# Layer weights' places lent to gathered keys, and a thinner interleave of attention at the layer border, in a two-layer graph transformer

## The chip, the cores and the metric

The kernel runs on one core of a Trainium2 chip. The metric is the device time of one launch in microseconds (us); the time of a version is the median of its runs. A profile is one execution recorded by the hardware profiler. PE is the matrix engine (TensorE), DVE the vector engine, ACT the scalar engine, POOL the general engine (GpSimd), which also issues the gathers, and SP the engine that issues most plain transfers.

## What is computed

Two transformer layers over 2708 nodes of 512 features, 8 heads of 64, a feed-forward part of width 2048. Attention goes only to the neighbours that a sparse adjacency matrix names. Each layer does this (the two layers have weights of their own):

```
mask = adj.astype(jnp.float32) + jnp.eye(n, dtype=jnp.float32)
q = (h @ Wq.T + bq).reshape(n, N_HEADS, D_K)
k = (h @ Wk.T + bk).reshape(n, N_HEADS, D_K)
v = (h @ Wv.T + bv).reshape(n, N_HEADS, D_K)
scores = jnp.einsum('nhd,mhd->hnm', q, k) / jnp.sqrt(jnp.float32(D_K))
scores = jnp.where(mask[None, :, :] == 0, jnp.float32(-1000000000.0), scores)
attn = jax.nn.softmax(scores, axis=-1)
ctx = jnp.einsum('hnm,mhd->nhd', attn, v).reshape(n, D_MODEL)
attn_out = ctx @ Wo.T + bo
h1 = _layer_norm(h + attn_out, ln1_g, ln1_b)
ff = jax.nn.relu(h1 @ W1.T + b1) @ W2.T + b2
h2 = _layer_norm(h1 + ff, ln2_g, ln2_b)
```

## The kernel before

**Stages.** The kernel first turns the adjacency matrix into a list of at most 24 neighbours for each node, while PE computes the keys and values of layer 0 (kept as rows of 1024 numbers in the table `kv_d[0]`) and then the queries (`first_queries`). Nodes are sorted by the length of their lists, so each of the 22 tiles of 128 nodes has its own number of list places (`CAPS`, 22 down to 3; the last tile has 20 nodes). From there on the work goes by 11 blocks of two tiles (`blocks`; the loop variable is k), once for layer 0 and once for layer 1. The stretch between the two layers, in which layer 1's first queries are computed, is called the border here.

**Two strands.** PE's strand is dense: for each block, `attended` (the context transposed, times Wo, first norm), `turned` (the result transposed to `hT`), `feed_forward` (16 steps f, each four matmuls into `pf`, a relu on ACT into `ft`, and the second product into `a`), the second norm, and in layer 0 `keys_values`, which makes the next layer's keys and values of the block. The other strand is attention, which PE does not touch. `loads` gathers neighbour rows with POOL's indirect transfers (L982), two list places, a *chunk*, into one tile `kv` of 8 KB a partition. `Tile.weights` multiplies a chunk by the queries and sums by head on DVE (L1019, L1025, into `sc`); `Tile.weigh` takes exponentials on ACT (L1038, into `p`), scales the values half on ACT (L1045), half on DVE (L1051), and adds them up on DVE (L1058, into `acc`). L1058 is the last reader of a chunk's tile, so it frees the place for a later gather. `sums` and `divided` end a tile's attention (L1081, and L1089 on ACT into `cx`). 

**What sets the order.** `attend` is a generator, one step a chunk: step j takes the gathered chunk j, writes out its weights, and then `weigh` of chunk j-1, `sums` of j-2 and `divided` of j-3. `loads` runs EARLY = 3 chunks ahead of that in the program. `advance(x)` adds x to a credit and runs steps while credit is left; the main loop calls it once for each f (0.62 in layer 0, 0.72 in layer 1), and `through(k + 1)` at f = 10 runs whatever is missing of the next block's attention in one go. The orders of PE, ACT and SP are those of the program text throughout. POOL's is that of the text up to the end of block 0 of layer 0; DVE's during `first_queries` and at the border. In the rest a scheduler orders DVE and POOL when the kernel is built, by its own idea of when things are ready. Every engine's stream is fixed then: an engine waits at an instruction whose inputs are not there, and everything behind it waits too.

**Places in memory.** The chunks have KVB = 5 tiles with the tag `kv`. `keys_values` takes one of these five for the rows that it scatters (`kvs`). Each weight matrix has one place of its own in the pool `wts`: `wq`, `wk`, `wv` are 4 x 512 numbers a partition, 8 KB, the size of a chunk's tile. Wq of layer 0 is last read by `first_queries`; Wq of layer 1 is loaded into the place at (k, f) = (3, 2) of layer 0 on SP's queue, and first read at the border. Wk and Wv of layer 1 are loaded in block 0 of layer 0, and last read by the last `keys_values`, at the start of the border.

**The border.** PE computes queries: two right after layer 0, two after the last keys and values, four more of tiles loaded beforehand, six of tiles streamed in (`now.queries`), then `through(0)` and `attended` of block 0, then two more. Before each of the four and the six stands `advance(0.5)`, so attention chunks of layer 1 lie between the queries' evictions (L1226, from PSUM into `qs`) in DVE's stream. The queries' sums `q`, the transposes `tp` and the product `o` share three PSUM tiles (tag `g`) in turn: PE can begin the fourth only when DVE has emptied the first. `qs` has three places in the tag `row`, freed when SP has stored it to `q_d`.

Of the kernel before, what the change touches and what calls it, by code (L numbers as in the profile page):

```python
# [8 lines left out]
F32 = mybir.dt.float32  # L9
# [9 lines left out]
P = 128  # L19
DM = 512  # L20
# [3 lines left out]
NC = DM // P  # L24
# [12 lines left out]
SLOTS = 2  # L37
QB = 3
LAG = 3
KVB = 5  # L40
# [431 lines left out]
def by_edges(ctx: ExitStack, tc: tile.TileContext, x, xT, adj, layers, out, good):  # L472
# [13 lines left out]
    NL = len(layers)  # L486
# [10 lines left out]
    wts = ctx.enter_context(tc.tile_pool(name="wts", bufs=1))  # L497
# [8 lines left out]
    all_made = []  # L506
    at = None
# [22 lines left out]
    def matrix(w, name, tag, by=None):  # L530
        src = chunked(w[name])
        t = wts.tile([P, src.shape[1], src.shape[2]], F32, tag=tag, name=tag)
        if by:
            by.dma_start(out=t, in_=src)
            return t
        k = max(1, src.shape[1] // 4)
        for c in range(0, src.shape[1], k):
            nc.sync.dma_start(out=t[:, c : c + k, :], in_=src[:, c : c + k, :])
        return t
# [11 lines left out]
    def turned_row(col, name, scale):  # L551

        t = rows.tile([P, DM], F32, tag=name, name=name)
        dg = dn.tile([P, NC, P], F32, tag="row", name="dg", bufs=3)
        for c in range(NC):
            nc.vector.tensor_scalar(
                dg[:, c, :], ident, col[:, c : c + 1], scale, ALU.mult, ALU.mult
            )
        yield t
        pr = ps.tile([P, DM], F32, tag="g", name="pr")  # L560
        for c in range(NC):
            nc.tensor.matmul(pr[:, c * P : (c + 1) * P], ones, dg[:, c, :], start=True, stop=True)
        nc.vector.tensor_copy(t, pr)
# [8 lines left out]
    def finish(steps):  # L572
        for _ in steps:
            pass
# [6 lines left out]
    def size(g):  # L581
        return min(P, N - g * P)
# [398 lines left out]
    def gather(to, table, s):  # L981
        nc.gpsimd.indirect_dma_start(  # L982
            out=to,
            out_offset=None,
            in_=table[:, :],
            in_offset=bass.IndirectOffsetOnAxis(ap=s, axis=0),
            bounds_check=N - 1,
            oob_is_err=False,
        )
# [12 lines left out]
    def chunks_of(g):  # L1002
        S = CAPS[g]
        k = (S + SLOTS - 1) // SLOTS
        cuts = [-(-S * i // k) for i in range(k + 1)]
        return [(g, a, b - a) for a, b in zip(cuts, cuts[1:])]

    class Tile:
# [75 lines left out]
        def divided(self):  # L1084
# [6 lines left out]
                )  # L1091
            return cx

    def loads(n):

        ready = []
        for g, s0, c in (chunk for g in order for chunk in chunks_of(g)):
            r = size(g)
            kv = at.tile([P, SLOTS, 2 * DM], F32, tag="kv", name="kv", bufs=KVB)
            for s in range(s0, s0 + c):  # L1100
                gather(kv[:r, s - s0, :], kv_d[n], idx[:r, g, s : s + 1])
            ready.append(kv)
            if len(ready) > EARLY:
                yield ready.pop(0)
        yield from ready
# [267 lines left out]
    NB = len(blocks)  # L1373
# [50 lines left out]
    def advance(more):  # L1424

        nonlocal credit
        credit = min(credit + more, 1.5)
        while credit > 0 and len(got) < CXB - 1:
            cost = next(ahead, None)
            if cost is None:  # L1430
                break
            credit -= cost

    def through(k):

        while blocks[k][-1] not in got:
            next(ahead)

    got = {}
    ahead = attend(0, got)  # L1440
# [37 lines left out]
    for n in range(NL):  # L1478
        last = n == NL - 1
        nxt = None if last else Layer(n + 1, layers[n + 1])  # L1480
        if n > 0:
            streamed = now.queries(order[8 : 2 * AHEAD])
            got = {}
            ahead = attend(n, got)
            with tc.manual_schedule(engines={mybir.EngineType.DVE}):
                for _ in range(2):
                    now.query(*pool.pop(0))
                next(ahead)
                next(streamed)
                while pool:  # L1490
                    advance(0.5)
                    now.query(*pool.pop(0))
                for i in range(2 * AHEAD - 10):
                    advance(0.5)
                    next(streamed)
                through(0)
                early[n] = now.attended(blocks[0], got)
                next(early[n])
                for _ in blocks[0]:
                    next(early[n])  # L1500
                finish(streamed)
            now.load_w2(NFC // 2 - 1)
        *_, hs = early[n]
        hT = now.turned(blocks[0], hs)
        turning = projecting = None
        in_order = ExitStack()
        if n == 0:
            in_order.enter_context(tc.manual_schedule(engines={mybir.EngineType.Pool}))
        for k, block in enumerate(blocks):
            more = k + 1 < NB  # L1510
            asking = iter(())
            if n > 0 and k + AHEAD < NB:
                asking = now.queries(blocks[k + AHEAD])
            for f, zs in enumerate(now.feed_forward(block, hs, hT)):
                if f == NFC:
                    break
                if f in (5, 6, 7, 8) and behind:
                    next(behind)
                if more and f == 10 + (k + n == 0):
                    through(k + 1)  # L1520
                    projecting = now.attended(blocks[k + 1], got)
                    next(projecting)
                if more and f == 11 + (k + n == 0):
                    for hs_next in projecting:
                        advance(0.5 if k else 0.0)
                advance(PACE[n] if k else 1.1 if f < 11 else 0.4)
                if f in (0, 3, 7, 9):
                    next(asking, None)
                if more and f == NFC - 1:
                    finish(asking)  # L1530
                    hT = now.turned(blocks[k + 1], hs_next)
                if k == 0 and len(now.w1) < NFC // 2 and f % 2 == 0:
                    now.load_w1(len(now.w1), nc.scalar)
                    now.load_w2(len(now.w2), nc.scalar)
                if n > 0 and (k, f) == (0, 2):
                    now.load_second(1, temp)
                if not last:
                    if (k, f) == (0, 10):
                        now.load_next()
                        now.kv = [matrix(nxt.w, "Wk", "wk", nc.scalar)]  # L1540
                    if (k, f) == (0, 13):
                        now.kv.append(matrix(nxt.w, "Wv", "wv", nc.scalar))
                    if (k, f) == (3, 2):
                        now.wq = matrix(nxt.w, "Wq", "wq")
                    if f == 1 and k in (1, 3):
                        i, name, scale = (1, "bk", 1.0) if k == 1 else (0, "bq", DK**-0.5)
                        turning = turned_row(now.cols[i], name, scale)
                        rows_of = now if k == 1 else nxt
                        setattr(rows_of, name, next(turning))
                    if f == 3 and k in (1, 3):  # L1550
                        finish(turning)
                if not last and not more:
                    if f % 2:
                        nxt.load_w1(f // 2)
                        if f > 2:
                            nxt.load_w2(f // 2 - 1)
                    if f == 6:
                        nxt.load_first()
                        nxt.load_second(0, temp)
                    if f == 7:  # L1560
                        finish(ahead)
                        pool += nxt.preloaded(order[:8], temp)
            in_order.close()
            if not last:
                behind = now.keys_values(block, zs)
            if more:
                hs = hs_next
        finish(ahead)
        if last:
            checked()  # L1570
        else:
            nxt.wq = now.wq
            for _ in range(2):
                nxt.query(*pool.pop(0))
            nxt.kept()
            for g in order[:2]:
                own[g] = asked(n + 1, g)
            finish(behind)
            behind = None
            now = nxt  # L1580
# [63 lines left out]
```

## Time and profile before

| | before |
|---|---|
| median of 3 runs | 1966.08 us (1964.01 to 1967.41) |
| the profiled execution's own time | 1964.63 us |
| its span | 1962.9 us |
| mean granted PE clock | 0.989 |

Busy time by stretch, in us, from a table of stretches:

| stretch | what runs | length | PE | DVE | ACT | POOL | PE clock |
|---|---|---|---|---|---|---|---|
| 0 to 264 | lists, keys and values, queries | 264 | 258.2 | 178.2 | 104.8 | 79.6 | 1.00 |
| 264 to 345 | layer 0, block 0 | 81 | 69.0 | 63.2 | 40.2 | 43.3 | 0.89 |
| 345 to 1130 | layer 0, the rest | 785 | 771.8 | 487.1 | 379.4 | 310.9 | 1.00 |
| 1130 to 1230 | border | 100 | 92.3 | 47.6 | 19.6 | 26.8 | 0.97 |
| 1230 to 1830 | layer 1, with attention | 600 | 590.2 | 496.7 | 367.3 | 322.4 | 1.00 |
| 1830 to 1962.9 | layer 1, the end | 132.9 | 119.7 | 27.9 | 22.6 | 13.7 | 0.96 |

A row is read like this: of the 81 us of layer 0's block 0, PE was busy for 69.0, and over that stretch it was granted 0.89 of its full clock, so its matmuls there were also slower than elsewhere. DVE is the fullest of the other engines in layer 1 (83%), and none of the others is full over a whole stretch.

### The profile page before, as it was taken

The page shows a single profiled execution, that of the slowest core. Times are in us where ns is not written, and L with a number is a line of the kernel's source. Part 1 is how long each engine was busy: PE and PEld are TensorE (multiplying, and loading weights), DVE is VectorE, ACT ScalarE, POOL GpSimd, SP SyncE. Part 2 cuts the span into 40 slices and gives each one's busy share as a digit, 9 for nine tenths or more (in the row PEclk, how much of TensorE's full clock was granted, in tenths as well). Part 3 has the DMA queues.
Part 4 walks back from the last instruction along what each step waited for, and adds up shares of the span by engine and source line. Part 5 has one row for each costly group of instructions (what it writes and reads, how often), then busy time and mean ns, then how long its engine had stood idle before and what let it go on. Part 6 is the DMA issues. An engine that isn't in the chain of part 4 may idle for free. (4 is left out here: it accounts for less than half of the span.)

```text
span 1962.9 us, 20872 instructions
## 1 busy us (share of the span) xinstructions
PE 1901.0 (97%) x6162; PEld 1100.6 (56%) x6162; DVE 1300.8 (66%) x2142; ACT 933.8 (48%) x3219; POOL 796.8 (41%) x710
## 2 busy tenths in 40 slices
PE   8999988999999999999999998999999999999997
PEld 4444444565565655566556643556666566666664
DVE  5884587685867869659442036888688988877421
ACT  4660254564555655547332112756456765755410
POOL 3114635453555535425310022555347655644210
PEclk9999999999999999999999999999999999999998
DMA  9998766455655556546310646856455766554000
GB/s 327 352 311 307 258 211 235 161 166 189 202 161 199 188 186 227 161 150 204 130 43 27 230 162 215 298 174 217 153 177 198 247 214 209 186 190 154 34 11 13
DMA packets 131486, 366.92 MB, mean 187 GB/s; under 512 B 16668, under 2 KB 36988, under 8 KB 128654
## 3 DMA queue, kind: packets, MB, share of 16 engines
q0 software_dynamic: 69120, 246.35, 37.9%
q1 hardware_dynamic: 53332, 99.66, 14.9%
q10 hardware_dynamic: 8910, 19.48, 2.6%
q8 instruction: 50, 0.82, 0.2%
q14 instruction: 74, 0.61, 0.1%
HBM read 314.62 MB, written 50.83 MB: 186 GB/s over the span
## 5 line engine op out<-in xcount | busy, mean ns | idle before, releaser
L982 POOL DMA_INDIRECT kv<-kv_d,idx x420 | 546.1, 1300 | 475.9 <-DVE acc L1058 319.1
L1284 PE MATMUL a<-w,ft 128*128 128x512 f32 (+1 forms) x1408 | 669.9, 601 | 10.8 <-ACT ft L1304 9.5
L1296 PE MATMUL pf<-hT,w 128*128 128x256 f32 (+1 forms) x2816 | 636.3, 373 | 13.2 <-ACT ft L1304 8.8
L1296 PEld LDWEIGHTS pf<-hT,w 128*128 128x128 f32 x2816 | 521.1, 191 | 192.2 <-issue 107.3
L1284 PEld LDWEIGHTS a<-w,ft 128*128 128x128 f32 (+1 forms) x1408 | 256.5, 187 | 239.0 <-issue 201.4
L1304 ACT ACTIVATE ft<-pf,b 128x256 f32<-128x256 f32 (+1 forms) x352 | 158.5, 459 | 424.8 <-PE pf L1296 424.5
L1019 DVE TENSOR_TENSOR kv<-kv,q 128x1024 f32<-128x1024 f32 (+3 forms) x222 | 256.5, 1158 | 156.3 <-DMA kv<-kv_d,idx 103.7
L1045 ACT ACTIVATE kv<-kv,p 128x64 f32<-128x64 f32 x1232 | 311.0, 335 | 5.0
L1025 DVE TENSOR_REDUCE sc<-kv 128x16 f32<-128x1024 f32 (+3 forms) x222 | 255.2, 1154 | 1.4
L1058 DVE TENSOR_TENSOR acc<-acc,kv 128x1024 f32<-128x1024 f32 (+2 forms) x178 | 204.0, 1146 | 26.7 <-ACT kv L1045 25.9
L1118 POOL TENSOR_TENSOR rd<-va,mhalf 128x1 f32<-128x1 f32 (+1 forms) x88 | 85.4, 971 | 267.6 <-DVE va L1116 266.2
L1038 ACT ACTIVATE p<-sc,minus 128x8 f32<-128x8 f32 (+1 forms) x420 | 103.4, 295 | 161.1 <-DVE sc L1025 154.6
L569 PE MATMUL o<-wo,cT 128*128 128x512 f32 (+1 forms) x352 | 157.8, 601 | 3.7 <-DVE qs L1226 3.3
L1051 DVE TENSOR_TENSOR kv<-kv,p 128x512 f32<-128x512 f32 (+1 forms) x178 | 121.6, 684 | 52.8 <-ACT p L1038 52.7
L569 PEld LDWEIGHTS o<-wo,cT 128*128 128x128 f32 (+1 forms) x352 | 65.5, 187 | 92.2 <-issue 80.9
L1089 ACT ACTIVATE cx<-acc,su 128x64 f32<-128x64 f32 (+1 forms) x352 | 88.4, 333 | 42.6 <-DVE su L1081 33.9
L1316 DVE TENSOR_TENSOR h<-a,h 128x512 f32<-128x512 f32 (+1 forms) x44 | 29.7, 677 | 106.8 <-PE a L1284 106.7
L1122 DVE SCALAR_TENSOR_TENSOR h<-h,rd,ln_b 128x512 f32<-128x512 f32 (+1 forms) x88 | 65.9, 749 | 50.9 <-POOL rd L1118 50.9
L663 ACT ACTIVATE code<-aj 128x2708 bf16<-128x2708 int32 (+1 forms) x22 | 73.2, 3329 | 49.1 <-POOL aj L659 45.4
L1355 POOL DMA_INDIRECT kv_d<-kvs,ident_i x22 | 23.7, 1077 | 179.0 <-ACT kvs L1349 110.9
L666 DVE MAX8 tops<-code 128x8 f32<-128x247 f32 (+2 forms) x242 | 83.1, 400 | 19.3 <-ACT code L663 19.3
L1045 ACT ACTIVATE acc<-kv,p 128x64 f32<-128x64 f32 (+1 forms) x352 | 88.8, 334 | 1.4
(133 smaller groups left out, 1514.2 us busy)
## 6 DMA issues: line engine op xcount, KB each, us to landing
aj<-in_adj SPq DMA_DIRECT2D x21, 1354.0 KB, 8.0
kv_d<-kvs ACTq DMA_DIRECT2D x21, 512.0 KB, 5.6
w<-in_W SPq DMA_DIRECT2D x20, 512.0 KB, 4.8
xg<-in_xT SPq DMA_DIRECT2D x19, 512.0 KB, 8.8
kv<-kv_d,idx POOLq DMA_INDIRECT x420, 5.6
w<-in_W ACTq DMA_DIRECT2D x12, 512.0 KB, 8.9
q_d<-qs SPq DMA_DIRECT2D x22, 256.0 KB, 4.2
zT_d<-zT SPq DMA_DIRECT2D x22, 256.0 KB, 5.3
```

What stands on the lines that cost most here:

```text
L569: nc.tensor.matmul(o[:r], xs(c), wm[:, c, :], start=(c == 0), stop=(c == NC - 1))
L982: nc.gpsimd.indirect_dma_start(out=to, out_offset=None, in_=table[:, :], in_offset=bass.IndirectOffsetOnAxis(ap=s, axis=0), bounds_check=N ...
L1019: nc.vector.tensor_tensor(kv[:r, :c, :DM], kv[:r, :c, :DM], self.q[:r].unsqueeze(1).to_broadcast([r, c, DM]), ALU.mult,)
L1025: nc.vector.tensor_reduce(self.sc[:r, s0 : s0 + c, :], kv[:r, :c, :DM].rearrange("p s (h d) -> p s h d", d=DK), AX.X, ALU.add,)
L1038: nc.scalar.activation(p[:r, s, :], self.sc[:r, s, :], AF.Exp, bias=minus[:r, g, s : s + 1])
L1045: nc.scalar.activation(to[:, i, hd], kv[:r, i, DM + h * DK : DM + (h + 1) * DK], AF.Copy, scale=p[:r, s0 + i, h : h + 1],)
L1051: nc.vector.tensor_tensor(to[:, 0, :].rearrange("p (h d) -> p h d", d=DK), kv[:r, 0, DM:].rearrange("p (h d) -> p h d", d=DK), p[:r, s0, : ...
L1058: nc.vector.tensor_tensor(self.acc[:r, :c, :], self.acc[:r, :c, :], kv[:r, :c, DM:], ALU.add)
L1089: nc.scalar.activation(cx[:r, hd], self.acc[:r, 0, hd], AF.Copy, scale=self.su[:r, h : h + 1])
L1284: nc.tensor.matmul(a[:r], fts[f][:, c0 : c0 + r], self.w2[f // 2][:, f % 2, :], start=(f == 0), stop=(f == NFC - 1),)
L1296: nc.tensor.matmul(pf[:, :w], self.w1[f // 2][:, c, f % 2 * P : f % 2 * P + P], hT[:, c, :w], start=(c == 0), stop=(c == NC - 1),)
L1304: nc.scalar.activation(ft[:, :w], pf[:, :w], AF.Relu, bias=self.b1[:, f : f + 1])
```

## The change

Three edits.

1. `rows_of_keys` hands out the chunks' tiles. In layer 0, for the first chunk that is requested after `first_queries` has ended and for all later ones, it goes round six places: five times the tag `kv`, then the place `wq`. In layer 1 it goes round seven from the first chunk on: five times `kv`, then `wk`, then `wv`.
2. Wq of layer 1 is loaded at the start of the last block, (NB - 1, 0), after the rest of layer 0's attention has been written out, instead of at (3, 2).
3. At the border each query is preceded by `advance(0.4)` instead of `advance(0.5)`.

```
+    places = []
+
+    def rows_of_keys(n):
+
+        if n == NL - 1 and not places:
+            places.extend([None] * KVB + ["wk", "wv"])
+        elif n < NL - 1 and all_made and not places:
+            places.extend([None] * KVB + ["wq"])
+        tag = places[0] if places else None
+        if places:
+            places.append(places.pop(0))
+        if tag is None:
+            return at.tile([P, SLOTS, 2 * DM], F32, tag="kv", name="kv", bufs=KVB)
+        kv = wts.tile([P, NC, DM], F32, tag=tag, name="kv")
+        return kv.rearrange("p c n -> p (c n)").rearrange("p (s n) -> p s n", s=SLOTS)
+
     def loads(n):
...
-            kv = at.tile([P, SLOTS, 2 * DM], F32, tag="kv", name="kv", bufs=KVB)
+            kv = rows_of_keys(n)
...
                 while pool:
-                    advance(0.5)
+                    advance(0.4)
                     now.query(*pool.pop(0))
                 for i in range(2 * AHEAD - 10):
-                    advance(0.5)
+                    advance(0.4)
                     next(streamed)
...
-                    if (k, f) == (3, 2):
+                    if (k, f) == (NB - 1, 0):
+                        finish(ahead)
+                        places.clear()
                         now.wq = matrix(nxt.w, "Wq", "wq")
```

No instruction is added or taken away. In the built programs the streams of PE and ACT are the same as before, instruction by instruction; SP's differs only in the place of the four transfers of Wq; DVE's and POOL's hold the same instructions in another order from the first chunk on that the sixth place lets run ahead.

## The prediction

> **What bounds the kernel now.** The page first: PE is the bound, and the question is only what its 62 us of idle time are (1962.9 less 1901.0), and what the lowered clock adds.
>
> ```profile
> span 1962.9 us, 20872 instructions
> PE 1901.0 (97%) x6162; PEld 1100.6 (56%) x6162; DVE 1300.8 (66%) x2142; ACT 933.8 (48%) x3219; POOL 796.8 (41%) x710
> ```
>
> Then PE's waits by releaser: no wait is PE's own, all are small, and nearly all are for ACT and DVE, which carry attention beside the dense strand.
>
> ```profile
> engine line waited for: us in total, times, longest us
> PE a L1284 <- ACT ft L1304: 9.5, 9, 2.8
> PE pf L1296 <- ACT ft L1304: 8.8, 4, 3.5
> PE tp L1128 <- ACT cx L1089: 5.4, 3, 3.8
> ...
> PE tp L1128 <- DVE h L1122: 4.3, 2, 3.9
> PE o L569 <- DVE qs L1226: 3.3, 1, 3.3
> PE q L569 <- DVE qs L1226: 2.9, 2, 1.7
> ```
>
> Third, the timelines where these waits lie. In layer 1 one pattern comes back, here (ACT, then PE) at 1424:
>
> ```profile
> 1424.16 0.49 ACT L1038 ACTIVATE p<-sc,minus 128x8 f32<-128x8 f32 x2 [4.64 <-DVE sc L1025]
> 1428.52 0.46 ACT L1304 ACTIVATE ft<-pf,b 128x256 f32<-128x256 f32 x1
> ...
> 1431.83 3.70 PE L1284 MATMUL a<-w,ft 128*128 128x512 f32 x8 [1.62 <-ACT ft L1304]
> ```
>
> ACT stood 4.64 us at an exponential whose scores DVE had only just made, so the relu behind it was late, and PE waited. DVE was late because it first had to do both norms of the block; before them it had stood idle for 12.47 us (its L1051 at 1405.53), with no chunk to work on: POOL's next gather had waited 24.63 us (at 1409.27) for L1058 to free a tile. The same ACT wait stands at 1514.72 (6.32), 1622.75 (5.16), 1819.10 (4.67), and in layer 0 at 741.30 (5.04).
>
> Last the border:
>
> ```profile
> 1202.15 3.70 PE L569 MATMUL q<-wq,zT 128*128 128x512 f32 x8 [1.21 <-DVE qs L1226]
> 1205.78 1.01 PE L1128 MATMUL tp<-ident,cx 20*128 20x20 f32 x8
> 1210.07 6.30 PE L569 MATMUL o<-wo,cT 128*20 128x512 f32 x8 [3.27 <-DVE qs L1226]
> ...
> 1201.47 1.22 DVE L1226 SCALAR_TENSOR_TENSOR qs<-q,bq 128x512 f32<-128x512 f32 x2
> 1209.23 0.69 DVE L1226 SCALAR_TENSOR_TENSOR qs<-q,bq 128x512 f32<-128x512 f32 x1 [5.83 <-DMA q_d<-qs]
> ```
>
> Two evictions follow each other at 1201.47: the first of them was due from 1193.5, when its query was done, but stood behind chunk work. PE lost 1.21 us. Its `qs` was then stored late (SP at 1202.13), so the eviction three later waited 5.83 us for the place, and PE 3.27 us.
>
> **What the Trainium skill says.** "TensorE: Matmul & The Clock Gate", section "What's actually happening": PE falls to half rate after about 3.4 us idle and needs about 3.4 us of work to come back. The trace agrees, and earlier than that: after the 3.27 us above, eight products took 6.30 us against 3.70 for the eight at 1216.83. So a wait of about 3 us costs some 2.6 us more. "Perfetto Trace Analysis", section "Optimization Strategy": a gap that repeats on the engine that should be full can mean too few buffers. The pattern at 1424 is of that kind, one engine removed. The same page, "Summary: the profiler window per engine type": the shown window of a POOL-issued transfer ends with its descriptors, not with the data. Here a gather shows 1.3 us on POOL and lands 5.6 us after issue (median), so a chunk of two must be asked for about 7 us ahead.
>
> **The change, part by part.** In the built streams PE and ACT are unchanged; all gain or loss must come through DVE and POOL.
>
> *Border (0.4).* One eviction moves: the first of the two at 1201.47 now stands right after one L1025, ahead of L1051, L1019, L1058, L1025, L1066 and small ones. From 1195.34 it follows 0.6 (eviction) and 1.2 (L1025), thus at 1197.1. PE's next query starts when its predecessor ends, 1200.9: 1.25 gained. The store goes out at 1197.8 rather than 1202.13; the old one freed its place 7.1 us later, the new one then by 1204.9; the eviction needs its query (1204.4), so it ends by about 1205.6 and `o` can start at 1206 instead of 1210.07. Of that 4.1, 1.25 is counted; 2.8 is new. No 3 us gap, no half rate: 2.6. Sum 6.6. Ends: 1.2 (the store lands as late as before) and 7.2. I take 6.
>
> *Layer 1, seven places.* The weights of two more chunks (2 x 2.4 us of L1019 and L1025) move ahead of the norms, to where DVE idles 12.47, and the scores ACT asks for are there. PE's waits from 1230 to 1830 are 6.5 + 1.6 + 1.2 + 0.2 = 9.5 us, and after the 2.81 us wait at 1631 eight products took 5.40 instead of 3.70: 11.2 with that 1.7. Around 1523 to 1537 DVE is 97% busy (48.6 of 50 us), more places help little there: 2.8 stays. Left 8.4; I take 8. If the cover is gone, that is, the added weights wait for their gather ahead of the norms, the norms are late by up to 4.8 us, against a slack of 4.3 to 6.2 between L1122 and the transposes: about 0. Ends 3 and 11.
>
> *Layer 0 after block 0, six places.* One chunk's weights (2.4 us) move ahead, and one gather is asked for ahead of each scatter of keys and values, behind which POOL's gathers stood. Candidates: PE's wait for `kvs` (1.6, at 458; DVE had stood 4.57 and 1.43 for gathers just before it), for `hT` 2.2 and 0.9. The 3.8 at 636 stays: there ACT itself had only reached the tile's last step, in an order that is not changed. Sum 4.7; I take 4. Against it: in eight of ten blocks the second L1122 ends only 0 to 2.7 us before PE needs it. Where DVE idles ahead of the burst (13 to 15 us at 473, 554, 801, 881, 960) the added 2.4 us are covered. Ends -6 and 8.
>
> *Layer 0, block 0.* A loss. The first chunk in Wq's place is the sixth after the queries; before it nothing changes, so the waits of 2.8, 3.5 and 1.4 us at 277 to 300 stay. But the third chunk after that one now has its weights ahead of the block's first L1254: 1.2 + 1.2 us more, with a gather that lands at about 320, so DVE reaches L1254 at 324.1 instead of 321.85. Behind it POOL's two `xb` gathers now both stand ahead of the first L1118, so DVE waits some 1.5 us for it, less what moves away. I get the second L1122 at 336.4 instead of 333.06: PE's wait of 3.86 us grows by 3.3. Ends 0 and 5.
>
> *Wq's load* (four issues, 0.6 us each) goes past SP's zT and xb stores and comes at about 1065, landing in some 9 us (median of the four at 442); PE wants it at 1138.33. The places wait for readers done long before (queries end at 264, keys and values at 1160.3, the gathers into them come later). Cost 0.
>
> *New waits.* DVE's and POOL's reordered streams must lose somewhere; unseen, I take 2, between 0 and 6.
>
> Sum: 6 + 8 + 4 - 3.3 - 2 = 12.7. From the profiled execution's own 1964.63 that is 1951.9. The median of the runs is 1.45 higher; the forecast is 1966.08 - 12.7, about 1953.
>
> **Rivals.** *A. Only the border pays.* ACT's waits for scores return one or two chunks later, since ACT's and PE's order is fixed and DVE's total work is the same. For it: DVE is 83% busy in layer 1. Against: 12.47 us idle right ahead of the lack. Then 6 - 3 - 2 + 2 (some of the rest) = 3: 1963.
>
> *B. The norms become late in layer 0: slower.* In each of its blocks the added chunk's L1019 and L1025 stand ahead of L1254. If its gather lands late, the second L1122 slips by 2.4 us against slacks of 0.03, 1.4, 2.1, 0.06, 1.1, 2.1, 2.1, 2.7: 2.4 + 1.0 + 0.3 + 2.3 + 1.3 + 0.3 + 0.3 = 7.9 on PE; the two gaps near 2.4 that join other waits and block 0's add half-rate time, three times 2.6. With block 0's 3.3, 19 lost. It decides from a slip of about 1.5 us, and wins over the gains if layer 1 gives only its lower end: 6 + 3 + 4 - 19 - 2 = -8, 1974. Against: the idle stretches before the bursts.
>
> *C. The places are not in use in time.* If the sixth and seventh place only repeat what POOL's own in-order work (rd, q, xb, scatters) lets through, nothing is asked for earlier outside the border: 6 - 1, 1961. Against: POOL's largest wait, 319.1 us in total, is for L1058, the freeing of tiles.
>
> **How the numbers follow.** Main case 0.62 (1953, own range 1945 to 1960), A 0.13, B 0.13, C 0.12. About 0.2% (3.9 us) is what a measurement tells from no change: faster means below 1962.2, same up to 1970. Faster takes the main case, most of C (0.09) and part of A (0.05): 0.76. Same: the rest of A (0.08) and C (0.03) and 0.03 of B, 0.14. Slower: the rest of B, 0.10. The range 1944 to 1965 leaves out B, a little of A and a very good main case.
>
> **What would show it.** Right: no PE wait at `o` near 1210 and none at the query before; ACT's waits for L1025 in layer 1 (70.6 us there now) cut by more than half, and PE's 9.5 there to below 4; POOL's wait for L1058 far below 319; PE's wait for L1122 near 333 longer than 3.86. Wrong: PE's waits for L1122 or `hT` in layer 0 summing to over 12; DVE's wait for gathers (103.7) unchanged; ACT's waits for scores as long as before.

## The result, and the profile after

The changed kernel takes 1957.76 us (median of 13 runs, 1951.51 to 1961.80), the kernel before 1966.74 in the same series; the medians differ by 9.0 us. The recorded ratio is 0.9949, with an interval of 0.9939 to 0.9960, which is 7.9 to 12.0 us gained; the forecast was 13. In the profiled executions the span went from 1962.9 to 1950.7, 12.2 less, against 12.7 in the prediction's sum; the profiled execution of the kernel after (1952.56 us) was one of the two quickest of its 13.

The page of the kernel after (span; busy time and share of each engine):

```profile
span 1950.7 us, 20853 instructions
PE 1892.6 (97%) x6162; PEld 1100.7 (56%) x6162; DVE 1300.1 (67%) x2142; ACT 933.4 (48%) x3219; POOL 797.9 (41%) x710
```

(The 19 instructions fewer are semaphore waits of DVE, SP and ACT; the counts of the five engines are the same.) PE's idle time fell only from 61.9 to 58.1; the other 8.4 us are busy time: the same products took less, at a mean granted clock of 0.992 instead of 0.989. The total hides more than it shows, as PE's waits of the kernel after tell (us in total, times, longest):

```profile
PE tp L1144 <- DVE h L1138: 13.1, 5, 3.4
PE pf L1312 <- ACT ft L1320: 10.1, 4, 4.6
...
PE pf L1312 <- ACT hT L1149: 4.4, 4, 2.8
...
PE a L1300 <- ACT ft L1320: 3.2, 2, 1.8
PE q L569 <- DVE qs L1242: 2.6, 1, 2.6
PE q L569 <- DMA zT<-zT_d: 1.5, 1, 1.5
```

(Lines after 1093 have moved on by 16, those after 1559 by 18: L1122 is now L1138, L1226 is L1242, L1284 is L1300.) The waits of `a` for the relu are down from 9.5 to 3.2, but the transposes' waits for the norm, 4.3 before, are now the largest sum, 13.1. So one stretch paid for another.

To see which, PE is its own clock: its order is the same in both kernels, so the start of the same `o` product in two traces, subtracted, gives how far one kernel has come ahead, with all overlaps and half-rate stretches in it. By stretch, after minus before:

| from `o` to `o`, us of the kernel before | what runs | predicted | found |
|---|---|---|---|
| 313 to 394 | layer 0, block 0 | +3.3 | +3.0 |
| 394 to 1042 | layer 0, the rest | -4 | +1.5 |
| 1042 to 1267 | border | -6 | -4.1 |
| 1267 to 1868 | layer 1 | -8 | -12.0 |
| | new waits, place unknown | +2 | in the rows above |

**Layer 1** gave what it was to give, and more. The waits there, from tables of waits of 1230 to 1830, first the kernel before, then after:

```profile
POOL kv L982 <- DVE acc L1058: 186.7, 40, 24.6
...
ACT p L1038 <- DVE sc L1025: 70.6, 26, 6.5
```

```profile
POOL kv L982 <- DVE acc L1058: 138.0, 25, 29.5
...
ACT p L1038 <- DVE sc L1025: 5.2, 5, 3.4
```

ACT waited 70.6 us for scores in this stretch before, 5.2 now; POOL's wait for freed tiles fell from 186.7 to 138.0 only. PE's waits there sum to 2.3 instead of 9.5.

**Layer 0** got new waits. Around the worst place, first the timeline of the kernel before (POOL, then PE; start, duration, in brackets the idle time and what ended it), then that of the kernel after (DVE, POOL, then PE):

```profile
727.50 1.19 POOL L982 DMA_INDIRECT kv<-kv_d,idx  x1 [1.95 <-DVE acc L1058]
...
741.73 0.59 POOL L1118 TENSOR_TENSOR rd<-va,mhalf 128x1 f32<-128x1 f32 x1
...
744.19 1.04 PE L1128 MATMUL tp<-ident,h 128*128 128x128 f32 x8
...
752.63 7.17 PE L1296 MATMUL pf<-hT,w 128*128 128x256 f32 x32 [2.25 <-ACT hT L1133]
```

```profile
727.66 1.23 DVE L1019 TENSOR_TENSOR kv<-kv,q 128x1024 f32<-128x1024 f32 x1 [2.17 <-DMA kv<-kv_d,idx]
...
730.85 1.23 DVE L1058 TENSOR_TENSOR acc<-acc,kv 128x1024 f32<-128x1024 f32 x1
...
747.87 0.75 DVE L1138 SCALAR_TENSOR_TENSOR h<-h,rd,ln_b 128x512 f32<-128x512 f32 x1 [2.82 <-POOL rd L1134]
...
732.34 1.20 POOL L982 DMA_INDIRECT kv<-kv_d,idx  x1 [6.59 <-DVE acc L1058]
...
747.25 0.59 POOL L1134 TENSOR_TENSOR rd<-va,mhalf 128x1 f32<-128x1 f32 x1
...
748.68 0.66 PE L1144 MATMUL tp<-ident,h 128*128 128x128 f32 x4 [2.53 <-DVE h L1138]
...
757.30 8.86 PE L1312 MATMUL pf<-hT,w 128*128 128x256 f32 x32 [2.81 <-ACT hT L1149]
```

Read from the top: the added chunk's L1019 stands ahead in DVE's order and waits 2.17 us for its gather. Behind it is the L1058 whose end POOL waits for. POOL's run of five gathers, the first norm's `rd` and four more gathers, all in front of the second norm's `rd` (L1134), therefore starts at 732.34; before, the same run started at 727.50. The `rd` comes at 747.25 instead of 741.73, with PE only 1.4 us later than before, so the norm is late, PE waits twice (once before, 2.25), and the 32 products take 8.86 us instead of 7.17.

Block 0 of layer 0, PE's timeline before, then after:

```profile
333.12 1.11 PE L1128 MATMUL tp<-ident,h 128*128 128x128 f32 x4 [3.86 <-DVE h L1122]
```

```profile
331.49 1.11 PE L1144 MATMUL tp<-ident,h 128*128 128x128 f32 x4 [2.72 <-DVE h L1138]
336.01 1.11 PE L1144 MATMUL tp<-ident,h 128*128 128x128 f32 x4 [3.40 <-DVE h L1138]
```

One wait of 3.86 became two with 6.12 in sum. The second norm ended at 335.96; the prediction had 336.4.

**The border** lost its wait at `o` and has two others. PE, then DVE:

```profile
1194.97 5.27 PE L569 MATMUL q<-wq,zT 128*128 128x512 f32 x8 [2.55 <-DVE qs L1242]
1201.79 10.54 PE L569 MATMUL q<-wq,zT 128*128 128x512 f32 x24 [1.55 <-DMA zT<-zT_d]
...
1193.03 1.23 DVE L1019 TENSOR_TENSOR kv<-kv,q 128x1024 f32<-128x1024 f32 x1 [4.37 <-DMA q<-q_d]
1194.17 0.18 DVE L1081 RECIPROCAL su<-su 20x8 f32<-20x8 f32 x1
1194.29 1.41 DVE L1242 SCALAR_TENSOR_TENSOR qs<-q,bq 128x512 f32<-128x512 f32 x2
```

The evictions that PE waits for stand right behind an L1019 that waited 4.37 us for a query tile to come back from `q_d` (a reload; 3.09 in the kernel before).

### The profile page after: what moved, and what is told of

Its sections match the earlier page's. It is cut to its first block, busy times and chain, and to the rows that moved or that the text cites. A ratio compares the mean times of both kernels' runs of the same rounds, so it can differ in the third digit from the quotient of the medians.

```text
span 1950.7 us, 20853 instructions
## 1 busy us (share of the span) xinstructions
PE 1892.6 (97%) x6162; PEld 1100.7 (56%) x6162; DVE 1300.1 (67%) x2142; ACT 933.4 (48%) x3219; POOL 797.9 (41%) x710
## 4 chain that ended last, share of the span: by engine, by line
PE 54%; issue 3%; DVE 2%; POOL 1%; DMA 1%; ACT 1%; POOLq 0%; SPq 0%; DVEq 0%
PE a L1300 21%; PE pf L1312 21%; PE o L569 5%; PE q L569 2%; PE k L569 2%; PE v L569 2%; PE tp L1144 1%; POOL kv L982 1%; DVE kv L1019 0%; DVE sc L1025 0%; DMA zT<-zT_d 0%; DMA kv<-kv_d,idx 0%; ACT hT L1149 0%; ACT kv L1045 0%; DMA kv_d<-kvs,ident_i 0%
## 5 line engine op out<-in xcount | busy, mean ns | idle before, releaser
L982 POOL DMA_INDIRECT kv<-kv_d,idx x420 | 540.6, 1287 | 459.8 <-DVE acc L1058 265.3
L1300 PE MATMUL a<-w,ft 128*128 128x512 f32 (+1 forms) x1408 | 663.7, 597 | 3.2 <-ACT ft L1320 3.2
L1300 PEld LDWEIGHTS a<-w,ft 128*128 128x128 f32 (+1 forms) x1408 | 255.7, 186 | 226.4 <-issue 202.5
L1019 DVE TENSOR_TENSOR kv<-kv,q 128x1024 f32<-128x1024 f32 (+3 forms) x222 | 254.4, 1157 | 178.5 <-DMA kv<-kv_d,idx 147.3
L1025 DVE TENSOR_REDUCE sc<-kv 128x16 f32<-128x1024 f32 (+3 forms) x222 | 254.2, 1152 | 1.5
L1058 DVE TENSOR_TENSOR acc<-acc,kv 128x1024 f32<-128x1024 f32 (+2 forms) x178 | 203.8, 1145 | 22.4 <-ACT kv L1045 21.3
L1134 POOL TENSOR_TENSOR rd<-va,mhalf 128x1 f32<-128x1 f32 (+1 forms) x88 | 88.9, 1011 | 290.4 <-DVE va L1132 289.4
L1138 DVE SCALAR_TENSOR_TENSOR h<-h,rd,ln_b 128x512 f32<-128x512 f32 (+1 forms) x88 | 65.7, 747 | 49.0 <-POOL rd L1134 49.0
L569 PE MATMUL k<-wk,xg 128*128 128x512 f32 (+1 forms) x176 | 82.0, 610 | 5.4 <-DMA wk<-in_Wk 4.9
```

Of the source, the lines that this page charges most:

```text
L569: nc.tensor.matmul(o[:r], xs(c), wm[:, c, :], start=(c == 0), stop=(c == NC - 1))
L982: nc.gpsimd.indirect_dma_start(out=to, out_offset=None, in_=table[:, :], in_offset=bass.IndirectOffsetOnAxis(ap=s, axis=0), bounds_check=N ...
L1019: nc.vector.tensor_tensor(kv[:r, :c, :DM], kv[:r, :c, :DM], self.q[:r].unsqueeze(1).to_broadcast([r, c, DM]), ALU.mult,)
L1025: nc.vector.tensor_reduce(self.sc[:r, s0 : s0 + c, :], kv[:r, :c, :DM].rearrange("p s (h d) -> p s h d", d=DK), AX.X, ALU.add,)
L1058: nc.vector.tensor_tensor(self.acc[:r, :c, :], self.acc[:r, :c, :], kv[:r, :c, DM:], ALU.add)
L1134: nc.gpsimd.tensor_tensor(rd[:r], va[:r], mhalf[:r], ALU.pow)
```

## The experiments

All ratios are to the kernel before on the same chip. Before its first change each kernel runs the same program, yet the first 313 us of single executions differed by up to 8 us; so the stretches below are differences of `o` starts and not of spans, and even identical stretches of layer 0 scatter by a few us.

**Each edit alone, and without layer 0.** e1 has the places of layer 1 only, e2 the place of layer 0 only, e3 `advance(0.4)` only, e4 the change without its layer 0.

```
e1, e4:
-        elif n < NL - 1 and all_made and not places:
-            places.extend([None] * KVB + ["wq"])
...
-                    if (k, f) == (NB - 1, 0):
-                        finish(ahead)
-                        places.clear()
+                    if (k, f) == (3, 2):
e2:
-        if n == NL - 1 and not places:
-            places.extend([None] * KVB + ["wk", "wv"])
-        elif n < NL - 1 and all_made and not places:
+        if n < NL - 1 and all_made and not places:
e1, e2 also:
-                    advance(0.4)
+                    advance(0.5)
```

> Only the seven places in layer 1; layer 0, Wq's load and the border (0.5) as before. Theory P, each stretch's difference between the two profiles belongs to the edit made in that stretch: PE reaches block 0's o of layer 1 (1210 before) at the same time, and layer 1 gives 12.0 us, so about 12 us below before (ratio 0.994). Theory Q, layer 1's gain hangs on the chunks being in another position at the border's end (0.4 for 0.5): 6 us or less is left (ratio 0.997 or more). The step of the prediction (8 us) lies between.

> Only the sixth place in layer 0, with Wq's load at (NB - 1, 0); layer 1 has its five places, the border 0.5. P: a loss of 4.5 us, 3.0 in block 0 and 1.5 after it (ratio 1.002), with PE's waits for L1138 and hT between 660 and 760 again. Q, those waits near 750 with their half-rate stretch are a chance of the one execution: only block 0's 3.0 is lost, and the 4 gained that the prediction had come back, a ratio of 0.999 to 1.000.

> Only 0.4 for 0.5 at the border. The prediction's step: 6 us gained (ratio 0.997), PE's waits at o near 1210 and at the query before it gone and no new one. P: 4 us (ratio 0.998), and the wait of 2.6 us for an eviction near 1190 with its half-rate query comes with 0.4 itself. Q: that wait comes from the seven places (their gathers and scores among the evictions), so here it is 1.7 as before and 6 us are gained.

> The change without its layer 0: five places there and Wq's load at (3, 2); seven places in layer 1 and 0.4. P: 12 + 4 = 16 us gained, ratio 0.992, and clearly below the changed kernel, by 4.5. If the border's and layer 1's parts share one gain (Q): 12 or less, a ratio of 0.994 or more.

| | block 0 | rest of layer 0 | border | layer 1 | ratio, interval |
|---|---|---|---|---|---|
| the change | +3.0 | +1.5 | -4.1 | -12.0 | 0.9949, 0.9939 to 0.9960 |
| e1 layer 1's places | +0.9 | +3.1 | -3.8 | -12.1 | 0.9945, 0.9926 to 0.9964 |
| e2 layer 0's place | +2.6 | +2.2 | +0.7 | +0.3 | 1.0021, 1.0011 to 1.0031 |
| e3 0.4 | +1.0 | +0.8 | -7.8 | +1.5 | 0.9977, 0.9969 to 0.9986 |
| e4 layer 1's places, 0.4 | +0.9 | +0.8 | -1.6 | -11.0 | 0.9934, 0.9916 to 0.9952 |

Layer 1's 12 us come from its two places alone (e1), layer 0's place is a loss by itself (e2): theory P stands in these two. It falls at the border. There 0.4 alone gives 7.8 by the trace, not 4 (4.5 by the times), the places alone give 3.8 with the old 0.5, and the two together 1.6 to 4.1. They do not add; they collide. e3's border shows what is missing (DVE, then PE):

```profile
1193.42 1.23 DVE L1019 TENSOR_TENSOR kv<-kv,q 128x1024 f32<-128x1024 f32 x1 [1.87 <-DMA q<-q_d]
...
1195.36 3.70 PE L569 MATMUL q<-wq,zT 128*128 128x512 f32 x8 [0.39 <-DVE qs L1226]
1199.55 7.10 PE L569 MATMUL q<-wq,zT 128*128 128x512 f32 x16 [0.49 <-DMA zT<-zT_d]
1207.51 3.67 PE L569 MATMUL q<-wq,zT 128*128 128x512 f32 x8 [0.86 <-DMA zT<-zT_d]
```

The same L1019 waited 1.87 us for the reload there. From its issue to the L1019 the reload took 5.7 us in e3, 6.9 before and 7.7 in e2 (all five places), 7.7 in e1, 8.0 in e4 and 8.3 after the change (seven). In the 9.5 us from its issue POOL sent three gathers in e3 and six in the changed kernel. The number of gathers alone does not settle the reload's time: it was 7.7 us in e2 with three and 7.7 in e1 with five.

**Is it the gathers, and how many places are needed?** e5 is e4 with the added places held back until the border's text is over; e7 is e5 with one added place; e6 is e2 with layer 0's place held back until block 1.

```
e5, e7:
-        if n == NL - 1 and not places:
+        if widened and not places:
...
                 finish(streamed)
+            widened.append(True)
e7 also:
-            places.extend([None] * KVB + ["wk", "wv"])
+            places.extend([None] * KVB + ["wk"])
e6:
-        if n < NL - 1 and all_made and not places:
+        if n < NL - 1 and widened and not places:
...
+            if k == 1:
+                widened.append(True)
```

> e4, but the sixth and seventh place are lent only to chunks requested after the border's last query; until then five. Theory R, at the border the added gathers delay the reload of a query tile on the same DMA engines, the L1019 that waits for it holds up the evictions behind it, and PE loses 4 to 6 us of what 0.4 brings there: the border gives the 7.7 us that 0.4 gave alone, the wait of 2.6 to 2.9 us for the eviction near 1195 is under 1, and layer 1 gives its 12, together 19 to 20 (ratio 0.990). Theory S, the reload's time (5.7 to 8.3 us) is chance, or the places have their gain from the border itself: ratio as e4's, 0.993 or more.

> e2, but the sixth place of layer 0 is lent only from block 1 on. Theory T, the loss of layer 0 has two parts, block 0's order of gathers and norms (2 to 3 us) and norms that come late behind POOL's gathers near 667 and 748 (1 to 2 us): a ratio of 1.0005 to 1.001, block 0 as before, PE's waits for L1138 near 667 and 748 still there. Theory U, later blocks lose only because block 0 leaves the chunks in another position: ratio 1.000 or below, and those waits gone or as before.

> e5 with one added place (wk) in layer 1 instead of two. If one more chunk's weights ahead of the norms already covers the 4.6 to 6.5 us that ACT waits for scores there, nearly the whole 12 us stay (ratio within 0.001 of e5's, ACT's waits for L1025 after the border below 15 us against 70.6 before). If the prediction's count of two chunks (4.8 us) is what covers it, about half stays: ratio 0.993, ACT's waits near 35.

| | block 0 | rest of layer 0 | border | layer 1 | ratio, interval |
|---|---|---|---|---|---|
| e5 | +1.5 | +2.1 | -1.7 | -12.6 | 0.9935, 0.9922 to 0.9947 |
| e6 | +0.6 | -1.5 | -1.3 | -0.1 | 0.9975, 0.9964 to 0.9986 |
| e7 | +0.5 | -1.2 | -2.4 | -5.9 | 0.9955, 0.9943 to 0.9968 |

e5 went against theory R, or seemed to. But POOL's order is not the text's at the border: in e5 too it sent six gathers in the 9.5 us after the reload, as its order there is the scheduler's. So e5 had not taken the gathers away, and decides nothing about them; e12 below takes them up again.

e7 answers the count: one place brings 5.9 us of the 12, and ACT's wait for scores from 1230 to 1830 falls to

```profile
ACT p L1038 <- DVE sc L1025: 25.6, 13, 6.7
```

against 70.6 with none and 5.4 with two (e5). It needs both.

e6 is a surprise: held back until block 1, layer 0's place is no loss but a gain of 0.25% (4.9 us), and its interval and e2's do not meet. So most of what layer 0 loses hangs on the place being lent in block 0. How much the place gains by itself is less sure: by the trace only 0.9 us of it lies in layer 0 and 1.3 at the border. Neither theory fits in full: the time is below U's 1.000, but T's wait for the norm near 667 is still there (2.79), and only the one near 748 is gone.

**The two transfers at the border.** e8 is e4 with the reload asked for one chunk earlier, so that it is no longer behind two more stores on SP. e9 is the changed kernel with layer 0's place from block 1 on, e10 the two together.

```
e8, e10:
-                if i > 0 and q is None and g != order[-1]:
+                if (i > 0 or (n, g) == (1, order[1])) and q is None and g != order[-1]:
e9, e10:
-        elif n < NL - 1 and all_made and not places:
+        elif n < NL - 1 and widened and not places:
```

> e4, with one thing moved: the query tile of the third tile of layer 1 is asked for back from q_d one chunk earlier, so on SP its transfer stands behind one store of queries instead of three. DVE's, PE's and ACT's orders are e4's. Theory R2, at the border the late landing of this reload (8.0 us after its issue in e4, 5.7 in e3) holds up L1019 and with it the evictions behind: now PE's waits near 1195 and 1202 (2.9 and 3.6 us in e4, then half rate) fall below 1 each, the border gives some 7 us instead of e4's 1.6, ratio 0.990 or 0.991. Theory S2, the zT loads are late by themselves among the gathers: PE's wait near 1202 stays at 3 us or more, the border gives 2 to 4, ratio 0.992 or 0.993.

> The changed kernel, with the sixth place of layer 0 lent only from block 1 on (as in e6). If block 0 is what layer 0 loses, and the rest of layer 0 gains 2 to 4 (e6), this is 5 to 8 us below the changed kernel: ratio 0.991. If e6's gain was the border's or a chance, the time is e4's: 0.993.

> e9 with e8's earlier reload. If the two are independent their gains add: 5 us at the border on top of e9, ratio 0.988 or 0.989; if e8's theory S2 holds, e9's time.

| | block 0 | rest of layer 0 | border | layer 1 | ratio, interval |
|---|---|---|---|---|---|
| e8 | +0.1 | +1.7 | -5.0 | -12.0 | 0.9924, 0.9910 to 0.9937 |
| e9 | +0.1 | -1.9 | -3.9 | -10.0 | 0.9913, 0.9899 to 0.9926 |
| e10 | +0.7 | -3.0 | -3.6 | -12.2 | 0.9892, 0.9876 to 0.9908 |

e9 came in as expected. In e8 the first wait is gone and the second stayed, so R2 and S2 were each half right (SP, then PE):

```profile
1188.78 0.38 SPq L1227 DMA_DIRECT2D zT<-zT_d  x1
...
1196.22 12.23 PE L569 MATMUL q<-wq,zT 128*128 128x512 f32 x24 [3.31 <-DMA zT<-zT_d]
```

From issue to PE's start this zT took 7.4 us. With five places in layer 1 it took 3.8 before and in e3 (issued at 1190.07 and 1195.75, PE at 1193.84 and 1199.55) and 3.4 in e2 and e6; with seven, 6.4 after the change and in e1 and e9, 6.9 in e4, 7.3 in e10; with the places held back in the text alone, 7.7 in e5 and 6.8 in e7. It also undid the earlier reload in e10: its border is no better than e9's, since the first wait (2.81) went but the zT's grew from 1.65 to 3.36.

**Two ways to cure the zT.** e11 is e10 with the transfer ahead of a store on SP; e12 is e10 with the added places held back at the border and POOL there in the order of the text.

```
e11, in queries and query:
-                    self.query(tiles[i], zTs[i])
+                    self.query(tiles[i], zTs[i], lambda: streamed(i + 4))
...
+            then()
             self.kept()
e12:
-        if n == NL - 1 and not places:
+        if n == NL - 1 and border and not places:
...
-            with tc.manual_schedule(engines={mybir.EngineType.DVE}):
+            with tc.manual_schedule(engines={mybir.EngineType.DVE, mybir.EngineType.Pool}):
...
                 finish(streamed)
+            border.append(True)
```

> e10, with each streamed zT's transfer issued on SP ahead of the store of the query before it, instead of behind it. In e10 the transfer was issued at 1183.50, after a store that waits for an eviction at 1182.4, and took 7.3 us to PE's start, so PE waited 3.36 us and ran at half rate after it. Theory V, it is late because of where it stands on SP: now it goes out 3 to 4 us earlier, PE's wait near 1191 is below 1, and 4 to 5 us are gained on e10: ratio 0.987. If the place in `cT` frees only then, the wait and the time stay (0.989).

> e10, with the sixth and seventh place of layer 1 lent only to chunks requested after the border's last query, and POOL's order at the border that of the text, so that no such gather can be put ahead (in e5 some were). Theory R, the transfers of zT take 6.4 to 7.4 us instead of 3.8 because the added gathers keep the DMA engines full: now they take about 4, PE's wait near 1191 is below 1, ratio 0.987, and layer 1 still gives 12. Rival, the gathers of five places fill the engines as well: the transfer takes over 6, ratio 0.989 as e10.

| | block 0 | rest of layer 0 | border | layer 1 | ratio, interval |
|---|---|---|---|---|---|
| e11 | -0.9 | +0.1 | -8.6 | -12.2 | 0.9891, 0.9875 to 0.9908 |
| e12 | +0.9 | -1.6 | -7.3 | -12.0 | 0.9899, 0.9883 to 0.9916 |

In both the border gives what it should. In e11 no query waits at all any more. In e12 (SP, then PE):

```profile
1185.68 0.38 SPq L1229 DMA_DIRECT2D zT<-zT_d  x1
...
1190.77 7.10 PE L569 MATMUL q<-wq,zT 128*128 128x512 f32 x16 [0.54 <-DMA zT<-zT_d]
```

5.1 us for the same transfer, with the added gathers held back, instead of 7.3 in e10; it does not get down to 3.8. The hold did not last: POOL sent eight gathers between 1187.61 and 1199.53, and the next but one zT, issued at 1192.07, took 7.6 us to land. It landed 0.05 us before the eviction to which the profile puts down a new wait of 1.96 at 1199.83. The packets of the traces say the same: from the issue of this zT to PE's start POOL's queue moved 0.1 to 0.5 MB in the four kernels with five places (3.4 to 3.8 us), 0.6 in e12 (5.1) and 1.4 to 2.1 in the eight others (6.4 to 7.7; e11 apart), while the queue of the plain transfers moved 0.8 to 1.0 MB in all of them. But POOL's order changed together with the places, and the gathers were never changed alone, so that they slow the transfer is well supported and not strictly shown. In e11 the transfers stay as slow (6.7 us for the first) and are only asked for earlier, and that alone ends the waits.

By the times neither can be told from e10; the 5.0 and 3.7 us more at the border are the traces' alone. e11's median is 1942.48 against 1963.58 before (four and seven runs), about twice the gain of the change, as is e10's.

## Why the prediction was right, and where its steps were not

The direction and the time were right, but that the spans agree so closely (12.2 against 12.7) is partly luck: layer 1 gave 4.0 us more than its term, layer 0 after block 0 gave 5.5 less and the border 1.9 less, and 2 had been set aside for new waits.

- **Layer 1, "I take 8".** The mechanism was right, its size too small: 12.0, and in the nine kernels with two places between 10.0 and 12.6. Two things made it small. "Around 1523 to 1537 ... more places help little there: 2.8 stays": these waits went too; the scores ACT asks for there had been made earlier. And the sum took only the waits that the profile shows. A wait also breaks the overlap of one matmul with the next: at 1523.61 PE waited 1.20 us but came 1.36 later than the pattern, and the eight transposes from 1534.04, with waits of 1.63, took 3.68 us to the next product instead of 0.87, 1.2 beyond the waits. The image of the idle stretch was wrong as well: DVE's 12.47 us ahead of the burst are still there, to the hundredth, at 1405.96. Two more places do not fill it. They build up a lead of two chunks once and keep it: when PE starts the `o` products near 1336, 1407 and 1472, DVE has begun 29, 39 and 50 score sums (L1025) of layer 1 in the kernel before, 31, 41 and 52 after, and 30, 40 and 51 with one place (e7).
- **Border, "I take 6".** For the edit alone the mechanism held: no wait at `o`, the half rate there gone, 7.8 by e3's trace (bound 7.2; the wait of 1.74 us for an eviction at 1189.67, which the step did not count, fell to 0.39). In the changed kernel it was 4.1, because a reload and a zT come late there: e8, where PE's first wait goes with an earlier reload, shows the one, and e11 the other. That the seven places' gathers delay them is well supported for the zT, and open for the reload. The prediction had put 2 for new waits without a place; at the border alone they cost 3.7, the difference between e3 and the change. Its list of signs failed on one point here: there is no wait at `o`, but there is at the queries.
- **Layer 0 after block 0, "I take 4".** Wrong: no gain came, but +1.5, and with e2 +2.2 (the kernels with five places scatter from -1.2 to +3.1 there, so these two stretches alone don't show a loss). Two of the named waits did go (1.56 for `kvs`, 0.90 for `hT`), and 1.33 at 430 with them, but three new ones for the norm came, 1.82 near 420, 2.64 near 667 and 2.53 near 748, and where 2.25 had been, 2.81 with half rate. Near 748 it is rival B's mechanism, an added chunk ahead of the norm whose gather is late, at a part of B's price.

  The step had set B aside with "Where DVE idles ahead of the burst (13 to 15 us at 473, 554, 801, 881, 960) the added 2.4 us are covered". In these five blocks that held: no wait for a norm came. But in the blocks whose first norms start at 402, 649 and 729 in the kernel before, DVE's last long idle time ahead of them was only 2.9, 1.8 and 7.8 us, and the three new waits stand in just these. The sum put nothing against them.

  The waits are no chance of one execution: norm waits near 420 (1.5 to 2.2 us) and near 667 (1.1 to 3.6) stand in all seven kernels with six places in layer 0 and in none of the seven with five (0.7 at most). The norm also waits for POOL, whose run of gathers starts only when DVE has done an L1058, as the timeline near 732 shows. The prediction's own sign of error, over 12 us of PE's waits for the norm and `hT` in layer 0, was met (16.4 in all, 7.9 before), and DVE's waits for gathers rose from 103.7 to 147.3 us.
- **Block 0, "-3.3".** Right in place and size: 3.0 in the pair; the mean of the two kernels that lend the place there is 2.8, of the twelve others (the kernel before among them) 0.5, so 2.3 is the place's own.
- **Wq's load, 0.** Right as far as the runs show: PE waits for no Wq in any trace, and e2's border is within 0.7 us of before.

What stays open: why the rest of layer 0 is better when block 0 does without the sixth place. The place where it differs is known: a norm wait near 748 stands only in the two kernels that lend the place from block 0 on (2.53, and 3.87 in e2; at most 0.60 elsewhere). Over the rest of layer 0 the five kernels with the place from block 1 on stand at -1.6 on average (-3.0 to +0.1), the seven with five places at +1.0 (-1.2 to +3.1), the two with it from block 0 at +1.9. The times agree on the sign (e2 and e6; the change and e9, 0.9949 and 0.9913). In e9 the same L1019 near 722 waits 1.17 us instead of 2.17, in e6 0.34 and in e10 to e12 not at all; what decides this was not tried.

## What to carry to other kernels

More buffers for a strand beside the bound paid in layer 1, where an engine was asked for something that could have been made earlier, and their number set the lead (one place gave half, two gave all). But each also lets transfers go earlier, and in a fixed order the new work stands in front of something: here of a small transfer that another engine needed soon, and of norms. So when a buffer is added, look at which short transfers and which short instructions lie in the stretch that the new requests move into, and try to issue those first, as e11 did. And where idle time is to cover the added work, look for it in every block: here five of eight had it, and the three without it paid.

## What was unexpected of the hardware

A transfer of 256 KB by SP took 3.4 to 3.8 us to its reader in the kernels with five places in layer 1 and 6.4 to 7.4 in those with seven, though the DMA engines were nearly full in both (busy share over the transfer 0.86 in e2, 0.92 before and 0.99 in e3, 1.01 after and 1.03 in e10). The Trainium skill, "TensorE: Matmul & The Clock Gate", section "What's actually happening", puts the fall to half rate at about 3.4 us of idle time. Here shorter waits were followed by it, and not always. Eight `a` products at one place (PE, e4 and e8):

```profile
1629.46 5.40 PE L1298 MATMUL a<-w,ft 128*128 128x512 f32 x8 [1.91 <-ACT ft L1318]
```

```profile
1619.63 3.70 PE L1298 MATMUL a<-w,ft 128*128 128x512 f32 x8 [1.73 <-ACT ft L1318]
```

The granted clock over these eight was 0.68 in e4 and 1.00 in e8: 1.7 us more after a wait of 1.91 than after one of 1.73. Yet in e4 eight queries took 3.70 after a wait of 2.91, and in e1, after one of the same length, 5.40. In these traces a wait of 2 to 3 us may or may not cost 1.7 us more behind it.
